# A filling queue that may go further into debt, and a reordered ending, in a GroupNorm, attention and projection kernel

## The chip, the core and the metric

The kernel runs on one NeuronCore of a Trainium2 chip, as one program. The metric is the device time of one execution in microseconds (us), the median of three runs. All the engines are named as the profile names them: PE is TensorE's matrix multiply, PEld its weight load, DVE is VectorE, ACT is ScalarE, POOL is GpSimd and SP is SyncE, which here only issues DMAs. A `q` behind an engine's name (SPq, ACTq) marks what its sequencer does itself, such as issuing a DMA, loading a register or branching. Times in the traces are counted from the start of the profiled span.

## The reference

```
x: (4, 512, 48, 48) float32, so batch 4, 512 channels, t = 2304 positions; 8 heads of 64 channels
hn  = group_norm(x, 32 groups) * scale + bias
qkv = einsum('oc,bchw->bohw', qkv_w, hn) + qkv_b, cast to float16
w   = softmax(einsum('bhct,bhcs->bhts', q*s, k*s)),  s = 1/sqrt(sqrt(64))
a   = einsum('bhts,bhcs->bhct', w, v), cast to float32
out = x + einsum('oc,bchw->bohw', proj_w, a) + proj_b
```

## The kernel before

**The stream.** A batch has four pairs of heads, so there are 16 pairs (g = 0 to 15). A pair's queries are cut into five blocks (j = 0 to 4), four of 512 columns and one of 256. A block is worked off in steps, six for a wide block and three for the narrow one, 27 steps for a pair and 432 in all (`stream`, n = 0 to 431). In step n, PE computes six score matmuls (`scores`, L955), twelve narrow ones in block 4, into three PSUM tiles `ps`; ACT turns them into `p` with three exponentials (L962); DVE adds `p` up (`add`, L1009); and PE multiplies the `p` of step n-2 with v (`values`, L980). PE runs its instructions in the order in which they were written, and so do ACT, DVE, POOL and SP. An engine waits for another one by semaphores alone, so that POOL may run a conversion long before or after the step of PE in which it was written.

**What is put between.** Everything else of PE's work, the projections to q, k and v (L709, L760) and the output projection (L844), is cut into pieces, which stand in one list `beside` in a fixed order. In each step `fill(n)` takes pieces from its front. A piece has a price in nominal microseconds, a first step `after` before which it may not be taken, and two marks, `first` and `last`, that say whether it begins or ends an accumulation chain. A whole chain carries both marks. At each call the credit grows by `rate`, the price of the pieces left over the steps left, and a piece's price is taken off when it is issued. A fill never begins a second chain after it has closed one.

```
        credit[0] = min(credit[0] + rate, 4.0)
...
            if us > 0.1 and credit[0] < us / 2:
                break
```

An output projection is a whole chain at 512/290 = 1.766 of those units (eight matmuls of 512 columns, `whi` and `wlo` for each of the four pairs). For the last three blocks of batch 3 it is cut in two: `FIRST`, the first three pairs (1.324 units), and `LAST`, the last pair alone (0.441 units, two matmuls). Four chains belong to a wide block, two to the narrow one. Before a block's first chain stands a piece of price 0, its conversion `att32`, which copies the attention of each pair c from float16 into the float32 tile `a32_c` that the chain's matmuls of that c read. Pairs 0 and 1 are copied by ACT (L838), pairs 2 and 3 by POOL (L836). There is one tile for each c, so that a copy waits for the chains of the block before that read it. The conversions of the last two blocks of batch 3 (`left_over`) have tiles of their own.

**Sums and division.** When a block's last `values` are done, its softmax sums go through DRAM: a copy, a DMA `sums` (L1051), on POOL the check of their range (L1070), on DVE a reciprocal (L1077), a DMA to a row (L1079), two broadcast DMAs `ib` (L1089), and on POOL the product `att` (`divide`, L1096), written six steps after the block's last one. POOL's queue takes that product, the checks and the conversions in the order in which they were written.

**The ending.** After step 431 the pieces that `beside` still holds are taken out as `ahead`, and the `LAST` chains not yet run are listed in `todo`: `ahead` first, then four of block 3 (tiles `rest`), then two of block 4 (tiles `held` and `last_av`). A chain of `ahead` is evacuated by a copy on ACT (L1424) and an add on POOL (L1427, in `finish`), the others by an add on DVE (L867). Each result is stored to `out` (L876), from SP or ACT in turn. POOL compares the block's sums with their range (L1456 to L1460), DVE and PE sum that up (L1470, L1471), and DVE writes `flag` (L1473). All five engines load the flag (L1488) and branch on it (L1494) past a fallback kernel, which with these inputs is not run. `expect_end` puts on an engine a register load of a zero (L923) and an announcement of that branch.

Of the kernel before, what the change touches and what calls it, by code (L numbers as in the profile page):

```python
# [17 lines left out]
ALU = mybir.AluOpType  # L18
# [8 lines left out]
P = 128  # L27
NC = C // P
# [439 lines left out]
def fast_path(  # L468
# [12 lines left out]
    nc = tc.nc  # L481
# [102 lines left out]
    def chain_bank(name):  # L584
        if alone[0]:
            return ps_s.tile([P, 2, QB], F32, tag="ps", name=name)[:, 0, :]
        return ps_w.tile([P, QB], F32, tag="pw", name=name)

    def small_bank(name):
        return ps_w.tile([P, QB], F32, tag="pw", name=name)  # L590
# [223 lines left out]
    def in_two(b, j):  # L814

        return b == B - 1 and j >= NQ - 3

    def left_over(b, j):

        return b == B - 1 and j >= NQ - 2  # L820

    beside_exps = range(NC // 2, NC)

    def att32(b, j, pairs=range(NC)):
        o, n = QBLOCKS[j]
        for c in pairs:
            if left_over(b, j):
                t = xpool.tile([P, n], F32R, tag=f"x{c}_{j}", name=f"a32_{b}_{j}_{c}")
            else:
                t = work.tile(  # L830
                    [P, QB], F32R, tag=f"a32_{c}", bufs=1, name=f"a32_{b}_{j}_{c}"
                )
            at32[b, j, c] = t[:, :n]
            source = atts[b * NPAIR + c][:, o : o + n]
            if c in beside_exps and len(pairs) > 1:
                nc.gpsimd.tensor_copy(at32[b, j, c], source)  # L836
            else:
                nc.scalar.copy(at32[b, j, c], source)  # L838
# [13 lines left out]
    FIRST, LAST = range(NC - 1), range(NC - 1, NC)  # L852
# [41 lines left out]
    def proj_pieces(b, j):  # L894

        def ahead(k):
            if k < len(proj_list) and not in_two(b, proj_list[k][0]):
                residual(b, *proj_list[k])  # L900

        def begin():
            att32(b, j, LAST if in_two(b, j) else range(NC))
            if j == 0:
                ahead(0)
                ahead(1)

        pairs = LAST if in_two(b, j) else range(NC)
        chains = [
            proj_piece(b, j, chunks, pairs, lambda k=k: ahead(k + 2))  # L910
            for k, (jj, chunks) in enumerate(proj_list)
            if jj == j
        ]
        return [piece(0.0, begin)], chains
# [6 lines left out]
    def expect_end(*engines):  # L921

        taken = nc.values_load(  # L923
            nothing[0:1, 0:1],
            engines=engines,
            min_val=0,
            max_val=1,
            skip_runtime_bounds_check_because="it is a constant",
        )
        tc.mark_branch_hint_location("fallback", taken, engines)  # L930
# [84 lines left out]
    def add_up(g, j, bank=None, more=False):  # L1015


        o, n = QBLOCKS[j]
        per = QB // n
        sl = bank  # L1020
        if bank is None:
            sl = ps_av.tile([P, QB], F32, tag="av", name=f"sl_{g}_{j}")
        steps = [
            (t, r, a)
            for t in acc.pop((g, j))
            for r in range(t.shape[1])
            for a in range(per)
        ]
        for i, (t, r, a) in enumerate(steps):
            for h in range(2):  # L1030
                lo = h * D
                nc.tensor.matmul(  # L1032
                    sl[lo : lo + D, :n],
                    ones16,
                    t[:, r, h, a * n : (a + 1) * n],
                    start=(i == 0 and (g, j) not in open_sums),
                    stop=(i == len(steps) - 1 and not more),
                )
        if more:
            acc[g, j] = []  # L1040
            open_sums.add((g, j))
        return sl
# [61 lines left out]
    beside = []  # L1104
# [34 lines left out]
    def do_tasks(room):  # L1139
        while tasks and tasks[0][0] <= now[0] and room > 0:  # L1140
            _, us, run = tasks.popleft()
            run()
            room -= us
# [42 lines left out]
    for b in range(B):  # L1186
# [20 lines left out]
        if b == B - 1:  # L1207
            put_qk(g + 3, 1)
            put_qk(g + 3, 0, range(NQ - 1))
            put_convert(old, 0)  # L1210
            put_qk(g + 3, 0, (NQ - 1,))

            ahead = [
                (residual, b, j, chunks)
                for j in (NQ - 2, NQ - 3, NQ - 1)
                for jj, chunks in proj_list
                if jj == j
            ]
            for j in range(NQ):
                put_proj(old, j, ahead)  # L1220
                if j + 1 < NQ:
                    put_convert(old, j + 1)

            for j in (NQ - 2, NQ - 3, NQ - 1):
                there = ends[(NG - 2) * NQ + j] + BEHIND + 6
                put_run(att32, b, j, FIRST, after=there)
                put_first(b, j)
            put_convert(b, 0)
            put_proj(b, 0)
            put_convert(b, 1)  # L1230
            put_proj(b, 1)
            put_convert(b, NQ - 3)
            put_proj(b, NQ - 3)
            continue
# [38 lines left out]
    for c in range(NC):  # L1273
# [10 lines left out]
        for i, chain in enumerate(chains):  # L1284
            evacuate = chain(c)
# [13 lines left out]
    credit = [0.0]  # L1299

    def issue():
        us, run = beside.pop(0)[:2]
        run()
        credit[0] -= us

    def fill(n):

        idle = beside and beside[0][4] and not beside[0][4]()
        if ended(n - 1):
            room = 1.1 if idle else 0.0
        elif ended(n - BEHIND - 1):
            room = 1.1 if idle else 0.5
        else:
            room = 2.4 if idle else 1.1
        do_tasks(room)
        rate, work = 0.0, 0.0
        for us, _, _, _, _, _, need in beside:  # L1320
            work += us
            left = min(need * per_pair, len(stream) - 4) - n
            rate = max(rate, work / max(left, 1))
        credit[0] = min(credit[0] + rate, 4.0)
        closed = False
        while beside:
            us, _, first, last, when, after, _ = beside[0]
            if after > n or (first and closed) or (when and not when()):
                break
            if us > 0.1 and credit[0] < us / 2:  # L1330
                break
            issue()
            closed = closed or last
# [21 lines left out]
    for n in range(end):  # L1355
# [10 lines left out]
        if summed:  # L1366

            fill(n)
# [10 lines left out]
        if not summed:  # L1379
            fill(n)  # L1380
        if n - BEHIND in soon:
            g, j = stream[n - BEHIND][:2]
# [9 lines left out]
    g, b, j = NG - 1, B - 1, NQ - 1  # L1392
    n = QBLOCKS[j][1]
    values(stream[-2])
    while loads:
        loads.popleft()[1]()
    check_sums(g, NQ - 2)
    att32(b, NQ - 2, LAST)

    def last_banks(name):  # L1400
        return ps_s.tile([P, 2, QB], F32, tag="ps", name=name)

    todo = [(jj, chunks) for jj, chunks in proj_list if in_two(b, jj)]
    todo = [k for k in todo if (k[0], k[1][0]) not in finished]
# [3 lines left out]
    add(stream[-1])  # L1408
    values(stream[-1])
    add_up(g, j, sl)  # L1410
    assert len(todo) == 8 and len(beside) == 2
    ahead, todo = todo[:2], todo[2:]

    def last_run(k, bank=None):
        return proj_run(b, *k, LAST, bank)

    def beyond(k, name, tag):
        bank = chain_bank(name)
        _, store = last_run(k, bank)
        t = xpool.tile([P, QB], F32, tag=tag, name=f"beyond_{name}")  # L1420
        xt = res[b, k[0], k[1][0]].rearrange("p m n -> p (m n)")

        def copy():
            nc.scalar.copy(t, bank)  # L1424

        def finish():
            nc.gpsimd.tensor_tensor(xt, t, xt, ALU.add)  # L1427
            store()

        return copy, finish  # L1430

    kinds = mybir.EngineType
    expect_end(kinds.DVE)
    inv = work.tile([P, QB], F32, tag="rows", name=f"inv_{g}_{j}")[:, :n]
    nc.vector.reciprocal(inv, sl[:, :n])
    o = QBLOCKS[j][0]
# [2 lines left out]
    copy, finish = beyond(ahead[0], "ahead_0", "x0_3")  # L1439
    copy()  # L1440
    expect_end(kinds.Pool)
    finish()
    ends_of = []
    for i, k in enumerate(todo[:NC]):
        if i % 2 == 0:
# [1 line left out]
        ends_of.append(last_run(k, banks[:, i % 2, :]))  # L1447
    expect_end(kinds.Activation)
    att32(b, j, LAST)
    copy, finish = beyond(ahead[1], "ahead_1", "x1_3")  # L1450
    copy()
    expect_end(kinds.PE, kinds.SP)

    every = fine.shape[1] + n
    fines = work.tile([P, QB], F32, tag="rows", name="fines")[:, :every]
# [2 lines left out]
    nc.gpsimd.tensor_scalar(ok, inv, 1.0 / SUM_MIN, None, ALU.is_le)  # L1458
    nc.gpsimd.tensor_tensor(fines[:, :n], fines[:, :n], ok, ALU.mult)
    nc.gpsimd.tensor_copy(fines[:, n:], fine)  # L1460
    finish()

    last_av = ps_av.tile([P, QB], F32, tag="av", name="last_av")
    for k, bank in zip(todo[NC:], (held[:, 1, :], last_av)):
# [1 line left out]
    good = small.tile([P, 1], F32, tag="good", bufs=1, name="good")  # L1466
    pf = small_bank("count")[:1, :1]
    for i, (evacuate, store) in enumerate(ends_of):
        if i == NC:
            nc.vector.tensor_reduce(good, fines, AX.X, ALU.add)  # L1470
            nc.tensor.matmul(pf, good, ones, start=True, stop=True)  # L1471
        if i == len(ends_of) - 1:
            nc.vector.tensor_scalar(flag, pf, P * every - 0.5, None, ALU.is_lt)  # L1473
        evacuate()
        store(nc.scalar if i % 2 else nc.sync)


@with_exitstack
# [54 lines left out]
```

## Time and profile before

| | us |
|---|---|
| median of three runs (1613.24 to 1616.65) | 1614.13 |
| the profiled execution's own time | 1613.1 |
| its span, from the first to the last instruction | 1611.4 |
| PE busy | 1581.6 |
| ACT busy | 1268.2 |
| DVE busy | 1136.2 |
| POOL busy | 321.5 |
| exponentials on ACT, mean of one | 1.025 |
| conversion of 128x512 on ACT, median from 1440 us on | 0.631 |
| conversion of 128x512 on POOL, median and longest from 1440 us on | 0.611 and 2.134 |

The profile is of one execution. Busy time is the union of an engine's instructions; a wide gap on PE means more than its share of busy time does, since nearly all of the span is PE's. An idle time is written in brackets in a timeline, with what ended it.

### The profile page before, as it was taken

The numbers are of one execution on the slowest core, as the hardware profiler recorded it, in microseconds if no ns is written. First come the engines' busy times: TensorE is split into PE (matmuls) and PEld (weight loads), VectorE is DVE, ScalarE is ACT, GpSimd is POOL, SyncE is SP. The second block draws the span as 40 slices with busy tenths as digits, with TensorE's granted clock in tenths as the row PEclk, the third lists the DMA queues.
The fourth block names the chain that finished last, engine by engine and source line by source line (L and its number), as shares of the span: only waits on it lengthen the run. The fifth ranks groups of instructions, "written<-read, shape, count | busy, mean of one in ns | idle before, by whom it ended". The sixth has DMA issues, their size and how long they took to land.

```text
span 1611.4 us, 28323 instructions
## 1 busy us (share of the span) xinstructions
PE 1581.6 (98%) x11500; PEld 695.2 (43%) x11500; DVE 1136.2 (71%) x1300; ACT 1268.2 (79%) x1362; POOL 321.5 (20%) x459
## 2 busy tenths in 40 slices
PE   7999999999999999999999999999999999999997
PEld 2533434443333534555333353455533334434554
DVE  6167668866666668986666666788666766667775
ACT  3077777888888888888887887887878888888895
POOL 1001112211121222312111121222212121222223
PEclk9999999999999999999999999999999999999998
DMA  7002020100000023511000001352100000016414
GB/s 219 4 14 67 11 66 22 18 14 11 14 18 14 10 68 119 158 50 28 14 12 18 14 12 57 100 157 79 27 16 14 14 15 14 12 31 183 129 53 140
DMA packets 94896, 82.10 MB, mean 51 GB/s; under 512 B 50852, under 2 KB 60964, under 8 KB 94756
## 3 DMA queue, kind: packets, MB, share of 16 engines
q1 hardware_dynamic: 92724, 78.35, 17.7%
q8 instruction: 92, 1.51, 0.4%
q10 hardware_dynamic: 1904, 1.84, 0.4%
q14 instruction: 48, 0.39, 0.1%
q0 software_dynamic: 128, 0.01, 0.0%
HBM read 60.70 MB, written 19.17 MB: 50 GB/s over the span
## 4 chain that ended last, share of the span: by engine, by line
PE 94%; DVE 2%; DMA 1%; ACT 1%; POOL 1%; issue 1%; SPq 0%; ACTq 0%; DVEq 0%; POOLq 0%
PE pqk L709 30%; PE ps L955 19%; PE av L980 19%; PE pv L760 16%; PE pr L844 8%; PE ps L709 1%; PE sl L1032 1%; ACT p L962 1%; DVE acc L1009 1%; DMA wqkv<-qkv_wT_dram 0%; POOL a L836 0%; DMA ib<-row 0%; DMA sums<-slx 0%; DMA row<-inv 0%; DMA x<-x_dram 0%
## 5 line engine op out<-in xcount | busy, mean ns | idle before, releaser
L962 ACT ACTIVATE p<-ps 128x1024 f16<-128x1024 f32 x1296 | 1233.4, 1025 | 311.6 <-PE ps L955 310.4
L1009 DVE TENSOR_TENSOR acc<-acc,p 128x3072 f16<-128x3072 f16 x270 | 485.9, 1800 | 70.8 <-ACT p L962 70.2
L709 PE MATMUL pqk<-x,wqkv 128*64 128x512 f32 (+1 forms) x2464 | 519.3, 551 | 0.0
L980 PE MATMUL av<-p,v 128*64 128x512 f16 (+1 forms) x2880 | 361.0, 364 | 0.4 <-DVE slx L1048 0.3
L955 PE MATMUL ps<-q,k 64*128 64x512 f16 (+1 forms) x2880 | 356.5, 358 | 1.7 <-ACT p L962 1.4
L760 PE MATMUL pv<-wqkv,x 128*64 128x256 f32 x2304 | 268.6, 380 | 0.0
L709 PEld LDWEIGHTS pqk<-x,wqkv 128*64 128x64 f32 x2464 | 169.0, 137 | 224.1 <-issue 166.7
L1070 POOL TENSOR_SCALAR in<-sums 128x8 f32<-128x8 f32 (+1 forms) x158 | 111.0, 703 | 718.9 <-DMA sums<-slx 712.4
L955 PEld LDWEIGHTS <-k 64*128 64x128 f16 x2880 | 106.3, 94 | 277.6 <-issue 228.8
L980 PEld LDWEIGHTS <-v 128*64 128x64 f16 x2880 | 132.0, 109 | 212.5 <-issue 168.4
L1096 POOL TENSOR_TENSOR att<-avx,ib 128x512 f16<-128x512 f32 (+1 forms) x78 | 122.8, 1575 | 446.1 <-DMA ib<-row 376.4
L760 PEld LDWEIGHTS pv<-wqkv,x 128*64 128x64 f32 x2304 | 160.6, 137 | 92.3 <-issue 4.5
L1009 DVE TENSOR_TENSOR acc<-p,p 128x3072 f16<-128x3072 f16 x79 | 138.2, 1749 | 0.0
L844 PE MATMUL pr<-a,whi 128*128 128x512 f32 (+1 forms) x310 | 122.3, 402 | 4.8 <-DVE q L719 2.1
L1012 DVE TENSOR_TENSOR acc<-acc 128x1024 f16<-128x1024 f16 x156 | 110.3, 707 | 5.3
L844 PE MATMUL pr<-a,wlo 128*128 128x512 f32 (+1 forms) x310 | 113.8, 375 | 0.0
L719 DVE TENSOR_SCALAR q<-pqk,bqkv 128x512 f16<-128x512 f32 (+1 forms) x79 | 54.8, 694 | 80.1 <-PE pqk L709 79.8
L719 DVE TENSOR_SCALAR k<-pqk,bqkv 128x512 f16<-128x512 f32 (+1 forms) x75 | 52.2, 696 | 77.9 <-PE pqk L709 77.8
L768 DVE TENSOR_TENSOR v<-pv,bv 128x512 f16<-128x512 f32 x72 | 49.7, 691 | 81.2 <-PE pv L760 80.9
L989 DVE COPY avx<-av 128x512 f32<-128x512 f32 (+1 forms) x79 | 50.6, 641 | 64.9 <-PE av L980 64.8
L871 DVE SCALAR_TENSOR_TENSOR r<-pr,bproj,r 128x512 f32<-128x512 f32 (+1 forms) x80 | 54.9, 695 | 46.2 <-PE pr L844 45.6
L844 PEld LDWEIGHTS pr<-a,whi 128*128 128x128 f32 x310 | 58.5, 189 | 43.8 <-issue 19.8
(79 smaller groups left out, 458.5 us busy)
## 6 DMA issues: line engine op xcount, KB each, us to landing
r<-x_dram SPq DMA_DIRECT2D x72, 256.0 KB, 3.2
out_dram<-r SPq DMA_DIRECT2D x69, 256.0 KB, 2.1
ib<-row SPq DMA_DIRECT2D x126, 128.0 KB, 3.1
x<-x_dram SPq DMA_DIRECT2D x62, 256.0 KB, 4.1
x<-x_dram SPq DMA_DIRECT2D x16, 128.0 KB, 4.8
sums<-slx SPq DMA_DIRECT2D x128, 2.0 KB, 2.1
ib<-row SPq DMA_DIRECT2D x30, 64.0 KB, 3.1
wqkv<-qkv_wT_dram SPq DMA_DIRECT2D x2, 768.0 KB, 6.9
```

The costliest lines, as they stand in the source:

```text
L709: nc.tensor.matmul(pw[0][lo : lo + D, :n], wqkv[:, c, w0 + lo : w0 + lo + D], hn[b, c, j], start=(c == 0), stop=(c == NC - 1),)
L719: nc.vector.tensor_scalar(qk[g][part][:, o : o + n], pw[0][:, :n], bqkv[:, col : col + 1], SCALE, ALU.add, ALU.mult,)
L760: nc.tensor.matmul(pw[0][lo : lo + D, a, :], hn[b, c, i * P // QB][:, at + lo : at + lo + D], wqkv[:, c, 2 * C + half * C // 2 :][:, : C / ...
L844: nc.tensor.matmul(ps[:, :n], w[:, c, bass.ts(m, P)], at32[b, j, c], start=(i == 0), stop=(i == len(steps) - 1),)
L871: nc.vector.scalar_tensor_tensor(xt[:, i], places[i], bias, xt[:, i], ALU.add, ALU.add)
L955: nc.tensor.matmul(ps[:, h, a * n : (a + 1) * n], kt[rows, bass.ts(i, P)], qt[rows, o : o + n], start=True, stop=True,)
L962: nc.scalar.activation(pt[:, r], ps, AF.Exp)
L980: nc.tensor.matmul(av[0][lo : lo + D, :n], vv[b, pr // 2][:, i, pr % 2 * P + lo : pr % 2 * P + lo + D], pt[:, r, h, a * n : (a + 1) * n], ...
L1009: nc.vector.tensor_tensor(t, before, pt, ALU.add)
L1012: nc.vector.tensor_tensor(t[:, 0], t[:, 0], t[:, r], ALU.add)
L1070: nc.gpsimd.tensor_scalar(t, sm, limit, None, op)
L1096: nc.gpsimd.tensor_tensor(atts[g][:, o : o + n], avx.pop((g, j))[:, :n], ibs.pop((g, j))[:, :n], ALU.mult,)
```

## The change

`att32` gives to POOL the copy of pair 3 that belongs to block 2 of batch 3 and was ACT's. In `fill`, a piece that is a whole chain is issued as soon as the credit is not negative; for the others the rule stays. The ending no longer asserts two chains in `ahead`, but one or two; where there is one, the second copy on ACT and add on POOL and its store fall away there, and where there are two, that store is put behind all the others. SP's announcement of the branch is written beside DVE's, ahead of the first store of the ending. In the last loop an evacuation and its store come before the sum of the comparisons, and the flag is written after the last evacuation.

```
-            if c in beside_exps and len(pairs) > 1:
+            if c in beside_exps and not (pairs == LAST and left_over(b, j)):
                 nc.gpsimd.tensor_copy(at32[b, j, c], source)
...
-            if us > 0.1 and credit[0] < us / 2:
+            if us > 0.1 and credit[0] < (0.0 if first and last else us / 2):
                 break
...
-    assert len(todo) == 8 and len(beside) == 2
-    ahead, todo = todo[:2], todo[2:]
+    ahead, todo = todo[: len(beside)], todo[len(beside) :]
+    assert len(todo) == NC + 2 and len(ahead) in (1, 2)
...
         def finish():
             nc.gpsimd.tensor_tensor(xt, t, xt, ALU.add)
-            store()
+            return store
...
-    expect_end(kinds.DVE)
+    expect_end(kinds.DVE, kinds.SP)
...
     expect_end(kinds.Pool)
-    finish()
+    finish()()
...
-    copy, finish = beyond(ahead[1], "ahead_1", "x1_3")
-    copy()
-    expect_end(kinds.PE, kinds.SP)
+    if len(ahead) > 1:
+        copy, later = beyond(ahead[1], "ahead_1", "x1_3")
+        copy()
+    expect_end(kinds.PE)
...
     nc.gpsimd.tensor_copy(fines[:, n:], fine)
-    finish()
+    if len(ahead) > 1:
+        store_ahead = later()
...
     for i, (evacuate, store) in enumerate(ends_of):
+        evacuate()
+        store(nc.scalar if i % 2 else nc.sync)
         if i == NC:
             nc.vector.tensor_reduce(good, fines, AX.X, ALU.add)
             nc.tensor.matmul(pf, good, ones, start=True, stop=True)
-        if i == len(ends_of) - 1:
-            nc.vector.tensor_scalar(flag, pf, P * every - 0.5, None, ALU.is_lt)
-        evacuate()
-        store(nc.scalar if i % 2 else nc.sync)
+    if len(ahead) > 1:
+        store_ahead()
+    nc.vector.tensor_scalar(flag, pf, P * every - 0.5, None, ALU.is_lt)
```

## The prediction

> **What bounds the kernel now.** I read the page's busy times and its chain first, then PE's timeline step by step from 1440 us on, since the queue's rule changes there, then the waits at each hole in PE, and last the instructions behind the last matmul.
>
> ```profile
> PE 1581.6 (98%) x11500; PEld 695.2 (43%) x11500; DVE 1136.2 (71%) x1300; ACT 1268.2 (79%) x1362; POOL 321.5 (20%) x459
> ...
> PE 94%; DVE 2%; DMA 1%; ACT 1%; POOL 1%; issue 1%; SPq 0%; ACTq 0%; DVEq 0%; POOLq 0%
> ```
>
> PE sets the time, and the change takes no matmul away. So it can gain only where PE stands still, and behind PE's end. Between 1440 and 1596 us PE has two large holes. Here is PE around 1463 us:
>
> ```profile
> 1462.98 0.39 PE L955 MATMUL ps<-q,k 64*128 64x512 f16 x2
> 1463.88 0.39 PE L955 MATMUL ps<-q,k 64*128 64x512 f16 x2 [0.51 <-ACT p L962]
> 1464.80 0.39 PE L955 MATMUL ps<-q,k 64*128 64x512 f16 x2 [0.53 <-ACT p L962]
> ```
>
> These are the scores of step 396. Step 395 holds scores and values alone, 1.52 us from 1461.46, whereas its three exponentials take 2.86 us: PE waits for ACT to free the tiles of `ps`. The other hole, with POOL's lines:
>
> ```profile
> 1486.69 1.27 POOL L1096 TENSOR_TENSOR att<-avx,ib 128x512 f16<-128x512 f32 x1 [8.49 <-DMA ib<-row]
> 1487.91 3.15 POOL L836 CAST a<-att 128x512 fp32r<-128x512 f16 x2
> 1490.10 0.50 PE L844 MATMUL pr<-a,whi 128*128 128x512 f32 x1 [1.18 <-POOL a L836]
> 1491.12 0.50 PE L844 MATMUL pr<-a,whi 128*128 128x512 f32 x1 [0.28 <-POOL a L836]
> ```
>
> A chain in step 402 waits for two copies, and these stood in POOL's queue behind a product that waited for its broadcast. Behind the last matmul I read what SP's queue waited for (us in all, times, longest) and the branch's rows (ns, then the first and last start):
>
> ```profile
> SPq L876 <- POOL r L1427: 2.8, 1, 2.8
> ```
>
> ```profile
> L1494 PEldq COMPARE_BRANCH  x1: 4107/4107/4107, 1603.3 to 1603.3; - x1
> ...
> L1494 ACTq COMPARE_BRANCH  x1: 68/68/68, 1604.6 to 1604.6; - x1
> L1494 SPq COMPARE_BRANCH  x1: 70/70/70, 1606.6 to 1606.6; - x1
> L1494 POOLq EVENT_SEMAPHORE  x1: 17/17/17, 1607.1 to 1607.1; - x1
> L1494 PEldq EVENT_SEMAPHORE  x1: 51/51/51, 1607.5 to 1607.5; - x1
> L1494 ACTq EVENT_SEMAPHORE  x1: 17/17/17, 1608.5 to 1608.5; - x1
> ```
>
> SP held finished results back until 1603.00. The semaphore lines are each engine's first act past the branch. SP's own comes at 1609.2 us, beside the landing of its last store (issued at 1604.4, 4.8 us to landing).
>
> **The credit.** I stepped the rule through the list in the code. It puts chains into the same steps as the trace's lines L709, L760 and L844, in every step to 430. At step 395 the credit is -0.8712. Left are 16 whole chains of block 0 to 4 of batch 2 (28.25 units), ten `FIRST` (13.24), eight whole ones of batch 3 (14.12), four `LAST` (1.77) and ten runs of 0.05 (0.50): 57.88 over 428 - 395 = 33 steps, a rate of 1.7539. The credit becomes 0.8827, and a chain asks 1.7655/2 = 0.8828: short by 0.0001, and the step stays empty. The new rule asks 0. Up to step 394 both rules issue the same; from 395 on every step takes what the next one took before. One `LAST` chain fewer is left: `ahead` has one entry, and the code for a second one (a copy on ACT, an add on POOL, the store to go last) is not run at all.
>
> **Step 395 filled.** Its chain takes 2.07 us (1459.39 to 1461.46 in step 394). ACT's exponentials end at 1464.75; the next scores come at 1462.98 + 2.07 = 1465.05 and wait for nothing. Scores of step 396: 2.14 us now (1462.98 to 1465.12), 0.75 elsewhere, **-1.39**.
>
> **Conversions a step earlier.** Block 2 of batch 2 is now converted in step 400 instead of 401, so it stands on POOL ahead of that product. The chain that frees its tiles ends at about 1483.3; two copies at 0.61 end at 1484.6; the next chain begins at 1484.8 and reads pair 2 first at 1485.7. The hole goes: 4.06 us (1487.72 to 1491.78) against 2.06, **-2.00**. What hides the copies is 1.5 us of scores and values. With DVE's adds beside them, as in the row above (2.13 for one), the 2.0 come back. Of the other moved conversions, only block 3's `FIRST` now comes right behind a product (step 410): by its row that broadcast lands 2.9 us into the step, the product takes 0.74 and the copy 0.61, 1520.5 us, and is read at 1522.3; nothing. ACT's two copies (1.26) come ahead of a 3.1 us step there: **+0.20** by ACT's 2.86 + 1.26 against 3.1 and the 0.8 us that its tiles reach ahead. From step 403 to 428 each step stands 2.07 - 1.39 - 2.00 = 1.32 us earlier, with one chain more done.
>
> **The late conversion on POOL.** It now reads a product that POOL itself has just written (1580.48 and 2.66 long; at most 1581.8 after the shift), and waits for the chain before, until 1581.7. Copy to 1582.4; read at 1583.2: **0**, slack 0.8. On ACT it stood ahead of exponentials (0.62). Bounds: -0.6, and +0.7 if it takes the 2.13 of the row above. [...] I take 0.61 because no `p` of block 3's last step is added on DVE, so DVE has only a PSUM evacuation then.
>
> **The last steps.** Steps 429 to 431 had one whole chain and two `LAST` (2.06 + 2 x 0.67); now three `LAST`, 2.01. Step 429 then takes PE 2.2 us against ACT's 2.86, and the third score tile of step 430 waits 0.65. To the end of `held`, 1596.27 us: -1.39 - 2.00 + 2.07 - 3.40 + 2.01 + 0.65 + 0.20 = **-1.9** us.
>
> **The ending.** From `held` to the flag (1602.72 + 0.14) the work keeps its order: reciprocal, product, four evacuations, POOL's three comparisons, sum. Flag at 1601.0. `held` is evacuated while DVE waited 0.87 for POOL, so the last evacuation ends at 1600.9 (before 1603.45) at no cost; the flag behind it still waits for the count, 0 to 0.1. SP's stores of `rest` and `held` go out by 1600, and only the flag's load (0.6) stands before its branch: 1601.65 instead of 1606.6. ACT: store at 1600.95, load, branch at 1602.0.
>
> Past the branch POOL takes 3.8 us, PE 4.1, ACT 3.9, SP 2.6, DVE 0.6. All had been announced (the L1529 hints behind the L923 loads), 5 to 7 us ahead, DVE's 9.8 us. So SP's earlier announcement, some 3.7 us by its queue, I cost at 0; its bounds are 0 and, since ACT comes as late, -1.0. ACT is past at 1605.95, PE at 1605.6, SP between 1604.2 and 1605.75, and the last store, 2.0 to 4.8 us after its issue, lands between 1603.0 and 1605.75. From SP's first semaphore to the end of the span are 1611.37 - 1609.21 = 2.16 us: 1606.4 to 1607.9. I take 1607.2, nearer to the longer rows since four engines fetch at once: **-4.2** on the span. The profiled execution would take 1613.1 - 4.2 = 1608.9; the median shown is 1.0 above it: 1609.9.
>
> [...]
>
> **Rivals.** *POOL's queue (slower).* Conversions in steps 396, 408, 410 and 428 now stand near a product or check. If the broadcasts land later than by these rows, each makes PE wait like step 402. It decides from 1.8 us at step 410 and 0.8 at 428; a broadcast took 5.0 us before step 402 and about 3 elsewhere. Four places at 2.0 to 2.5 against -4.2: +4 to +6, about 1619. Against it: loads of residuals made that one slow, and they are over by step 404. Chance 0.10.
>
> *The copies stay slow.* They meet DVE's adds wherever they stand, and step 401 waits as 402 did: the 2.0 us return, 1611.9, no difference. For it: 2.13 and 1.07 in the row. Against: the six other pairs from 1440 us on took 0.61 or less each. Chance 0.22.
>
> *The change does not do what it says.* 0.0001 may round the other way in my stepping, or two chains may remain; then only SP's order gains: ACT's branch resumes at 1608 and the end is 2.3 sooner, 1611.8. Chance 0.04.
>
> **How the numbers follow.** The sum above has 0.64; its own range is 1607.2 to 1611.5, from the branch's bounds, -1.0 for the announcement, +0.7 for the late copy and the runs' spread. About what a measurement of this kernel can tell from no change is 0.2%, 3.2 us: 1610.9 to 1617.4. Of the 0.64, 0.61 lie below that; with 0.02 of the second rival, faster has 0.63. The rest of the first case and of the two rivals near 1612 make 0.27, POOL's queue 0.10. The range reaches down to the first case's end and up to 1614.0, past the two middle cases, and leaves out POOL's queue and little else.
>
> **What would show it.** Step 395 has eight `pr` matmuls and step 396's scores no gap; no `pr` of step 401 waits for POOL's L836; POOL's 17 copies from 1440 us on become 18, ACT's 23 become 22; L1424 and the add of L1427 appear once; `held` ends near 1594.4, the flag stands near 1601, SP's branch near 1601.7, the span ends near 1607. I am wrong if another `pr` waits over 1 us for L836, if `held` ends after 1595.5, or if an engine needs over 5 us past its branch.

## The result, and the profile after

The kernel after took 1610.4 us (median of 20 runs, 1608.46 to 1613.69) against 1613.32 for the kernel before (20 runs, 1611.6 to 1617.17): a ratio of 0.998 [0.9973, 0.9987], 2.9 us less. A second set of 11 runs of the same kernel (`e5_after` below) gave 1609.58 against 1613.09, 0.9979 [0.997, 0.9988]. The profiled execution of after took 1612.11 us with a span of 1610.4, so it is one of the slower of its kernel; the profile of `e5_after`, with a span of 1608.3, stands beside it in what follows.

The page's busy times and the shares of its chain, after:

```profile
PE 1582.2 (98%) x11500; PEld 694.0 (43%) x11500; DVE 1136.0 (71%) x1301; ACT 1267.1 (79%) x1360; POOL 318.9 (20%) x459
...
PE 93%; DVE 2%; DMA 2%; issue 1%; ACT 1%; POOL 1%; SPq 0%; ACTq 0%; DVEq 0%; POOLq 0%
```

PE has as many matmuls and is as busy as before. ACT lost two instructions (the late copy and the second evacuation of `ahead`). So the gain has to be in the holes and in the end. PE's timeline of after, steps 395 and 396:

```profile
1461.59 0.82 PE L955 MATMUL ps<-q,k 64*128 64x512 f16 x6
1462.34 0.84 PE L980 MATMUL av<-p,v 128*64 128x512 f16 x6
1463.11 0.50 PE L844 MATMUL pr<-a,whi 128*128 128x512 f32 x1
...
1465.17 0.82 PE L955 MATMUL ps<-q,k 64*128 64x512 f16 x6
```

Step 395 now has its eight `pr` matmuls, and the six scores of step 396 stand in one line without a bracket: nothing waits for ACT. At the other hole, POOL's timeline from 1482 to 1491 us has two lines, and PE's step 402 has no bracket:

```profile
1483.18 1.17 POOL L836 CAST a<-att 128x512 fp32r<-128x512 f16 x2 [4.11 <-PE pr L844]
1487.36 1.27 POOL L1096 TENSOR_TENSOR att<-avx,ib 128x512 f16<-128x512 f32 x1 [3.01 <-DMA ib<-row]
```

The two copies that followed this product in the profile of before now run ahead of it, and are done by 1484.4. At the last matmuls, POOL's add no longer holds SP's queue. SP's waits from 1585 us on, before and then after (us in all, times, longest):

```profile
SPq L876 <- POOL r L1427: 6.2, 2, 3.3
...
SPq L1494 <- SPq L1494: 2.6, 1, 2.6
```

```profile
SPq L876 <- DVE r L867: 5.6, 4, 2.1
SPq L1497 <- SPq L1497: 4.8, 1, 4.8
...
SPq L876 <- POOL r L1427: 2.7, 1, 2.7
```

Of the two waits for L1427, 6.2 us together, one is left. It ends with POOL's only add at 1598.7, just ahead of the first evacuation of `rest` (1598.1 and 0.68 long), so it holds nothing back. Longer now is the wait of SP for itself past the branch (L1497, which was L1494): 4.8 us, 2.6 before. The branch's rows show it:

```profile
L1497 SPq EVENT_SEMAPHORE  x8: 17/17/17, 1608.3 to 1608.8; - x8
L1497 SPq COMPARE_BRANCH  x1: 70/70/70, 1603.4 to 1603.4; - x1
...
L1497 PEldq COMPARE_BRANCH  x1: 494/494/494, 1603.5 to 1603.5; - x1
L1497 ACTq COMPARE_BRANCH  x1: 68/68/68, 1604.0 to 1604.0; - x1
...
L1497 ACTq EVENT_SEMAPHORE  x1: 17/17/17, 1608.0 to 1608.0; - x1
L1497 POOLq EVENT_SEMAPHORE  x1: 17/17/17, 1608.2 to 1608.2; - x1
```

SP branches 3.2 us sooner than before (1606.6), but is past the branch only 0.9 us sooner (1609.2). POOL, which is off to the branch as early as before, needs 4.8 us where it needed 3.8.

The stages of the three profiles, each counted from the start of step 394, up to which the kernels are the same (us). The predicted column is the sum on record, stage by stage:

| stage | before | predicted change | after | `e5_after` |
|---|---|---|---|---|
| steps 395 and 396 | 6.48 | +0.68 | 7.17 (+0.69) | 7.17 (+0.69) |
| steps 397 to 402 | 23.84 | -2.00 | 21.90 (-1.94) | 21.92 (-1.92) |
| steps 403 to 428 | 91.27 | +0.20 | 92.72 (+1.45) | 91.48 (+0.21) |
| step 429 to the end of `held` | 13.21 | -0.74 | 12.53 (-0.68) | 12.53 (-0.68) |
| `held` to the flag | 6.60 | 0 | 6.62 | 6.61 |
| flag to the end of the span | 8.52 | -2.3 | 7.86 (-0.66) | 7.10 (-1.42) |
| sum | | -4.2 | -1.1 | -3.1 |

Two rows miss the forecast: steps 403 to 428 in the profile of after, and the last row in both. The experiments went after these two, and after the question which part of the change earns the time.

### The profile page after: what moved, and what is told of

Read it like the earlier page. It is cut to its first block, busy times and chain, and to the rows that moved or that the text cites. A ratio compares the mean times of both kernels' runs of the same rounds, so it can differ in the third digit from the quotient of the medians.

```text
span 1610.4 us, 28319 instructions
## 1 busy us (share of the span) xinstructions
PE 1582.2 (98%) x11500; PEld 694.0 (43%) x11500; DVE 1136.0 (71%) x1301; ACT 1267.1 (79%) x1360; POOL 318.9 (20%) x459
## 4 chain that ended last, share of the span: by engine, by line
PE 93%; DVE 2%; DMA 2%; issue 1%; ACT 1%; POOL 1%; SPq 0%; ACTq 0%; DVEq 0%; POOLq 0%
PE pqk L709 29%; PE ps L955 19%; PE av L980 19%; PE pv L760 16%; PE pr L844 8%; PE ps L709 1%; PE sl L1032 1%; DVE acc L1009 1%; ACT p L962 1%; DMA wqkv<-qkv_wT_dram 0%; DMA row<-inv 0%; DMA ib<-row 0%; POOL a L836 0%; DMA sums<-slx 0%; DVE r L871 0%
```

## The experiments

Each was timed in five rounds beside the kernel before. `e1_credit` to `e4_early_copy` shared a chip and the runs of before; so did `e5_after` to `e8_no_branch`, then `e9_early_words` and `e10_no_words`, then `e11_both` and `e12_before_words`.

### Which part gains, and the place of two copies

**The credit alone.** The kernel before with the new rule in `fill`. The `ahead` code was cut to its one remaining entry, and the rest is that of before.

```
-            if us > 0.1 and credit[0] < us / 2:
+            if us > 0.1 and credit[0] < (0.0 if first and last else us / 2):
```

> The credit rule alone: one chain left in ahead, so the second copy, add and store fall away by themselves, while the late copy stays on ACT, SP's announcement stays behind its store and the last loop keeps its old order. Theory 1 (the credit rule carries the change: it fills step 395, moves the copies of step 402 out of the way, and by leaving one chain it also frees SP's stores): both holes in PE gone (1.39 and 2.00 us), a new wait of about 1 us in step 411 for POOL's copy behind the product, SP's stores out by 1601.7; 2.0 to 2.6 us under the kernel before, ratio near 0.9985. Theory 2 (the rewritten ending carries it): the loop's gain is eaten by step 411 and the starved steps 430 and 431, under 0.8 us, ratio 0.9995 to 1.0.

Measured: 1610.24 us, 0.9984 [0.9975, 0.9993]. It has the whole gain of the change, within what can be told apart. One chain fewer is left for `ahead`, and that alone takes POOL's second add, and SP's wait for it, out of the ending: SP branches at 1601.2 and POOL at 1601.0, without any of the edits made to the ending.

**Everything but the credit.** The kernel after with the old rule.

```
-            if us > 0.1 and credit[0] < (0.0 if first and last else us / 2):
+            if us > 0.1 and credit[0] < us / 2:
```

> Everything of the change except the credit rule: two chains in ahead, their second store last on SP. Theory 1: step 396's scores and step 402's chain wait as before (0.5 + 0.5 and 1.18 + 0.28 us), the held tile still ends near 1596.2 us; SP's stores of rest and held go out up to 1.5 us sooner, but POOL's add still ends near 1603.0 and its store follows it, and the engines that miss the branch's target need 4 us: 0 to 1.5 us under the kernel before, ratio 0.999 to 1.0. Theory 2: 2 to 3 us under it, ratio near 0.998.

Measured: 1612.5 us, 0.9997 [0.9988, 1.0006]: no difference. PE waits at both holes as before, 1.1 us in all at the second where it was 1.5 (from 1440 us on):

```profile
PE ps L955 <- ACT p L962: 1.4, 3, 0.5
PE pr L844 <- POOL a L836: 1.1, 2, 0.8
```

Its ending gains nothing either: 8.75 us from the flag to the end, 8.52 before. SP does branch sooner (1604.9, against 1606.6 before), but ACT and POOL then need over 5 us past the branch (ACT 1604.3 to 1609.5, POOL 1604.1 to 1609.7).

**The late copy back on ACT.** The kernel after, with the condition in `att32` that of before.

```
-            if c in beside_exps and not (pairs == LAST and left_over(b, j)):
+            if c in beside_exps and len(pairs) > 1:
```

> The changed kernel with the late copy of pair 3 back on ACT. Theory 1: ACT waits for the chain of step 428 with it, copies for 0.62 us and starts step 429's exponentials 0.2 us later, so that the third score tile of step 430 waits 0.7 to 0.9 us instead of 0.52; 0.2 us slower than the changed kernel (0 to 0.6), ratio to the kernel before near 0.998. Rival (POOL's copy matters, since ACT is what bounds steps 429 to 431): 0.6 us or more slower, a wait of over 1.1 us in step 430.

Measured: 1610.03 us, 0.9982 [0.9973, 0.9991], no difference from `e5_after`. The trace does show a small one: from step 429 to the end of `held` it takes 12.78 us, and 12.77 in `e1_credit`, which has the copy on ACT too, against 12.53 with the copy on POOL. So the move is worth 0.25 us, which is too little for the runs' times to show. This profile also shows the collision of the next experiment: step 411, which took 3.11 us in `e5_after`, takes 3.92 here.

**Block 3's first conversion a step sooner.** In the profile of after, the excess of 1.24 us over `e5_after` in steps 403 to 428 is in the main one place: step 411 took 4.37 us against 3.11, the step behind it 0.24 less, and step 403 0.22 more. POOL's timeline at step 411:

```profile
1521.15 0.72 POOL L1096 TENSOR_TENSOR att<-avx,ib 128x256 f16<-128x256 f32 x1 [7.52 <-DMA ib<-row]
1521.82 2.14 POOL L836 CAST a<-att 128x512 fp32r<-128x512 f16 x1
```

and PE's, in step 411:

```profile
1522.63 0.40 PE L844 MATMUL pr<-a,wlo 128*128 128x512 f32 x1
1524.01 0.50 PE L844 MATMUL pr<-a,whi 128*128 128x512 f32 x1 [0.98 <-POOL a L836]
```

The same two instructions of POOL in `e5_after`:

```profile
1519.82 0.73 POOL L1096 TENSOR_TENSOR att<-avx,ib 128x256 f16<-128x256 f32 x1 [6.49 <-DMA ib<-row]
1520.49 0.61 POOL L836 CAST a<-att 128x512 fp32r<-128x512 f16 x1
```

and what DVE did meanwhile, in after and then in `e5_after`:

```profile
1521.21 2.28 DVE L1009 TENSOR_TENSOR acc<-acc,p 128x3072 f16<-128x3072 f16 x1
```

```profile
1520.92 1.80 DVE L1009 TENSOR_TENSOR acc<-acc,p 128x3072 f16<-128x3072 f16 x1
```

DVE's add begins 4.5 us into step 410 in every profile. In `e5_after` the copy was two thirds done by then, and took 0.61 us. In after the broadcast landed about 1 us later; the copy began 0.6 us into the add and ended 0.47 us behind the add's end (1523.96 against 1523.49), 2.14 us in all. The product began 4.4 us into step 410 there, 4.0 in `e3_copy_act` (copy 2.15), and 3.2 to 3.5 in the other profiles of this order, whose copies took about 0.6. The experiment writes this conversion into POOL's queue ahead of the product:

```
+                if j == NQ - 1:
+                    there = ends[(NG - 2) * NQ + NQ - 2] + BEHIND + 6
+                    put_run(att32, b, NQ - 2, FIRST, after=there)
...
-                put_run(att32, b, j, FIRST, after=there)
+                if j != NQ - 2:
+                    put_run(att32, b, j, FIRST, after=there)
```

> The changed kernel with the conversion of block 3's first three pairs put two chains earlier in the list (issued in step 409 instead of 410), so that POOL has it ahead of the product of step 410 that waits for its broadcast. Theory 1 (step 411's wait is POOL's order): the pr of step 411 waits for nothing, the 2.1 us copy of pair 2 becomes one of 0.6, step 412 begins 1.2 us sooner and the held tile ends 1.0 to 1.2 us sooner; about 1.1 us faster than the changed kernel, ratio to the kernel before near 0.9973. Rival (something else is late by as much: ACT's two copies, or the evacuations): the wait moves to the exponentials of steps 410 to 412 and the time stays, ratio near 0.998.

Measured: 1609.44 us, 0.998 [0.9971, 0.9989]. Step 411 took 3.11 us. In a later kernel with this order (`e11_both`) the product began 4.1 us into step 410, and step 411 still took 3.11. So the order removes the collision. Of the nine profiles with the order of after, two show it (after and `e3_copy_act`), so the profile of after was probably an unlucky one. The medians can't tell: that of `e4_early_copy` is 0.14 us under that of `e5_after`, and each ratio is uncertain by about 0.1%, 1.5 us.

### The ending, part by part

**The kernel after itself,** unchanged, for a second profile and a median on this chip:

> The changed kernel itself, for a second profile and a time beside the next three. If step 411's wait hangs on when the broadcast lands, as in the two profiles with and without it, it comes out at some other length, 0 to 1.3 us, here; if it is fixed by the order alone, it is 1.0 us again. Both holes of before stay gone, the third score tile of step 430 waits 0.5 us. 2.5 to 3.5 us under the kernel before, ratio 0.998.

Measured: 1609.58 us, 0.9979 [0.997, 0.9988], `held` at 1594.6. Its branch:

```profile
L1497 SPq EVENT_SEMAPHORE  x8: 17/17/17, 1606.2 to 1606.7; - x8
L1497 SPq COMPARE_BRANCH  x1: 70/70/70, 1602.2 to 1602.2; - x1
...
L1497 PEldq COMPARE_BRANCH  x1: 3723/3723/3723, 1602.3 to 1602.3; - x1
```

PE's branch took 3.7 us here and 0.5 in the profile of after, in one and the same program.

**SP's announcement beside PE's again:**

```
-    expect_end(kinds.DVE, kinds.SP)
+    expect_end(kinds.DVE)
...
-    expect_end(kinds.PE)
+    expect_end(kinds.PE, kinds.SP)
```

> The changed kernel with SP's announcement of the branch back beside PE's, behind SP's first store. Theory 1 (the earlier announcement brings nothing): SP is 2.6 to 4.9 us past its branch, as with it, and the time is within 0.5 us of the changed kernel's, or up to 1 us better, since the credit rule alone, with the announcement here, had 6.6 us from flag to end and not 7.3 to 7.9. PE, which crossed its branch in 0.5 us where it was announced alone and in 4 us where it was announced together with SP, needs 4 us again. Theory 2 (it brings what it was written for): SP needs 1 to 2 us more past its branch, 1 us slower.

Measured: 1609.67 us, 0.9976 [0.9967, 0.9986]. SP passed its branch in 3.9 us (1602.1 to 1606.0), against 4.0 in `e5_after`. The announcement's place in the ending makes no difference.

**The last loop in its old order,** the comparisons' sum and the flag ahead of the last evacuations:

```
-        evacuate()
-        store(nc.scalar if i % 2 else nc.sync)
...
+        if i == len(ends_of) - 1:
+            nc.vector.tensor_scalar(flag, pf, P * every - 0.5, None, ALU.is_lt)
+        evacuate()
+        store(nc.scalar if i % 2 else nc.sync)
...
-    nc.vector.tensor_scalar(flag, pf, P * every - 0.5, None, ALU.is_lt)
```

> The changed kernel with the last loop in its old order: the count before the evacuation of held, the flag before the last evacuation. Theory 1: the flag is written at the same place, since it hangs on POOL's comparisons; the last evacuation ends 0.6 us later and its store with it, but it lands before the engines are past their branches: 0 to 0.3 us. Theory 2: the last store sets the end, 0.6 us slower.

Measured: 1610.03 us, 0.9978 [0.9969, 0.9987]. No difference.

**No branch:** the loads of the flag, the announcements and the branch are gone.

```
-    fails = nc.values_load(
...
-    with tc.If(fails > 0, label="fallback"):
-        general_path(tc, *args)
```

> The changed kernel without the flag's loads, the announcements, the branch and the fallback behind it (the flag is still computed). Theory 1 (the engines' way past the branch sets the end): from flag to the end of the span 4.5 to 5.5 us instead of 7.3 to 7.9, bounded by the last store's landing and SP's list of semaphores; 2 to 3 us faster than the changed kernel, ratio to the kernel before 0.996 to 0.997. Rival (the landing of the last stores sets it): within 0.5 us of the changed kernel.

Measured: 1606.02 us, 0.9954 [0.994, 0.9967]. From the flag to the end are 3.73 us instead of 7.10. Five runs make this median. It is 3.6 us under that of `e5_after`, and the flag's loads with the branch are the cause, since the announcements alone cost nothing (`e10_no_words` below); the rest of the tail (last stores, the end of the program) stays.

### When an announcement is of use

In every kernel so far with a branch DVE, announced first, was past it in 0.6 us, and SP, ACT and POOL never in less than 2.6. The page of after lists two DMA queues of the kind `instruction` (packets, MB, share of 16 engines):

```profile
q8 instruction: 92, 1.51, 0.4%
...
q14 instruction: 48, 0.39, 0.1%
```

The packets of q8 are of 16 KB, those of q14 of 8 KB. The last of 8 KB ahead of the branch (1603.4) came at 1501.7, 1518.3, 1526.6 and 1595.7, the last of 16 KB at 1595.0 and 1599.7. So DVE's announcement (1593.2) had one more packet of 8 KB behind it, SP's, ACT's and POOL's, at 1595.9 to 1597.3, had none, and PE's (1597.1) had one of 16 KB. Which engine a packet is for the trace does not tell; the engines that the next expectation names are my inference from the packets' size and from the engine's place in its code.

**Announced earlier:** SP, ACT and POOL at step 400, PE at step 430, DVE where it was.

```
+        if n == 400:
+            expect_end(kinds.SP, kinds.Activation, kinds.Pool)
+        if n == 430:
+            expect_end(kinds.PE)
...
-    expect_end(kinds.DVE, kinds.SP)
+    expect_end(kinds.DVE)
```

and without the later three.

> The changed kernel with the announcements of SP, ACT and POOL put into step 400 and PE's into step 430, DVE's where it was. In the traces an engine's code arrives in blocks, and the last blocks before the branch were fetched near 1501 (POOL), 1518 (SP), 1526 (ACT), 1594 (PE) and 1594 us (DVE); only DVE was announced before its fetch, and only DVE crossed its branch in 0.6 us every time. Theory A (an announcement is served by the engine's next block fetch): all five engines are past the branch within 0.7 us, no block fetch lies between branch and first semaphore, from flag to the end of the span 4.0 to 5.0 us instead of 7.0 to 8.2, 2 to 3 us faster than the changed kernel, ratio to the kernel before near 0.996. [...]

Measured: 1607.15 us, 0.9966 [0.9954, 0.9978]. The branch:

```profile
L1498 SPq EVENT_SEMAPHORE  x8: 17/17/17, 1601.2 to 1602.7; - x8
L1498 SPq COMPARE_BRANCH  x1: 70/70/70, 1600.7 to 1600.7; - x1
...
L1498 PEldq COMPARE_BRANCH  x1: 504/504/504, 1600.8 to 1600.8; - x1
...
L1498 POOLq EVENT_SEMAPHORE  x1: 17/17/17, 1601.3 to 1601.3; - x1
L1498 ACTq EVENT_SEMAPHORE  x1: 17/17/17, 1601.4 to 1601.4; - x1
```

All five engines are past it within 0.6 us, and no packet of the two instruction queues comes between the branch and that: the next one comes at 1601.8. The span ends 4.52 us after the flag.

**No announcements at all,** the branch kept:

```
-    expect_end(kinds.DVE, kinds.SP)
...
-    expect_end(kinds.Pool)
...
-    expect_end(kinds.Activation)
...
-    expect_end(kinds.PE)
```

> The changed kernel with no announcement at all, the branch kept. Theory A: only DVE loses by it (its crossing takes 3 to 5 us like those of the others), and as SP, ACT and POOL take as long anyway, from flag to end 7 to 8 us as in the changed kernel: within 0.5 us of it, ratio to the kernel before near 0.998. Theory B (the late announcements do help those engines): 1 us or more slower than the changed kernel.

Measured: 1609.6 us, 0.9979 [0.997, 0.9988], as after. The row that tells is DVE's:

```profile
L1493 DVEq COMPARE_BRANCH  x1: 72/72/72, 1600.3 to 1600.3; - x1
...
L1493 DVEq EVENT_SEMAPHORE  x1: 21/21/21, 1604.3 to 1604.3; - x1
```

Without its announcement DVE needs 4.0 us where it needed 0.6. So the announcements do work, and those of the kernel after bring nothing to SP, ACT and POOL; removing them costs nothing. What the early ones changed is both the place ahead of the 8 KB packets (those at 1501.7 to 1526.6 in after) and the time ahead of the branch, over 100 us instead of 3.6 to 8.4. For SP, ACT and POOL no run separates the two. For PE the time ahead does not decide: announced 5.1 to 6.6 us ahead, it passed in 0.5 us in five profiles and in 3.7 to 4.1 in four.

**Both,** the early announcements with the early conversion of `e4_early_copy`:

> Both improvements on the changed kernel: the announcements of SP, ACT, POOL and PE put ahead of their last block fetches, and block 3's first conversion issued in step 409. Expected 0 to 0.3 us better than the announcements alone (the collision in step 411 came in two of ten profiles of the order it removes, at 0.8 and 1.2 us): 1606.5 to 1607.5, ratio to the kernel before near 0.996. Rival: the copies of ACT that now fall into step 409 cost as much elsewhere, no difference.

Measured: 1607.16 us, 0.997 [0.9958, 0.9982]. Its edit is the sum of the two above. It shows no gain over `e9_early_words`, timed in another set (0 to 0.3 us were expected). The two are the best of those that keep the branch: `e9_early_words` is 2.4 us under `e10_no_words` of the same set, and both are some 6 us under the kernel before.

**The kernel before with the early announcements:** the edit of `e9_early_words` on the old credit and ending.

> The kernel before, with the announcements alone put ahead of the last block fetches. Its ending has a second bound, the store behind POOL's last add, so that SP issues its last store 1.5 us behind the flag and it lands 6 us behind it. Theory 1 (two bounds lie side by side in the kernel before, and the credit rule took away only the one): all engines past the branch in 0.6 us, but from flag to end still 7.5 to 8.5 us, 0 to 1 us faster than the kernel before, ratio 0.9995 to 1.0. Rival (the branch alone bounds both kernels): 2.5 us faster, ratio 0.9985.

Measured: 1612.23 us, 0.9997 [0.9988, 1.0006], no difference. PE, ACT and POOL are past the branch in 0.5 us, and yet from the flag to the end are 8.71 us. SP's waits from 1585 us on:

```profile
SPq L876 <- POOL r L1432: 6.7, 2, 3.5
...
SPq L1495 <- SPq L1495: 3.0, 2, 2.4
```

SP's last store still stands behind POOL's second add; its packets run until 1606.6, and the second of SP's two waits past the branch ends at 1607.0. The span ends 2.4 us behind the last packet of a store here, in the profile of before, and in `e1_credit`, `e9_early_words` and `e11_both` (2.3 to 2.4), but 4.2 us or more behind it in after and the other profiles with a branch. So SP's store set the end of before, with the branch close by (ACT is past it at 1608.5, SP goes on at 1609.2), and to take away the branch's cost alone gives nothing. To take the store away gave 0.7 us in the profile of after and 1.9 in that of `e1_credit`, from flag to end. The change takes the store away (by the credit); the early announcements then take the branch. This profile shows one thing more: step 402 took 4.11 us here, 5.59 in the profile of before and 3.58 in after. The product on POOL had begun at 1484.74 (1486.69 there), and PE waited 0.27 us for the copies, although one of them still took 2.13. So that hole, too, grows and shrinks with the landing of a broadcast: this slow copy began 0.48 us into an add of DVE's, the one of before 0.94, and both ended 0.47 us behind the add.

## Why the prediction was right, and where it missed

**The credit and step 395: right.** The traces show chains in the steps that the stepping of the rule gave, up to step 430. Steps 395 and 396 changed by +0.69 against +0.68, and one entry of `ahead` is left. `e1_credit` and `e2_no_credit` together show that this rule is the cause of the gain.

**Conversions a step earlier: right, with one place more.** Step 402 lost its 2.0 us (5.59 to 3.58), and the two copies moved ahead of its product took 0.61 and 0.62 in after. Step 411 was the exception. The prediction had seen its copy come behind a product, and cleared it by a slack of 1.8 us. The copy has to begin before DVE's add does, 4.5 us into the step, to take the 0.61 of `e5_after` and not the 2.14 of after; it comes 0.67 us behind the product's begin, which may thus lie 3.8 us into step 410, where the row of before gave 2.9. The true slack is 0.9. The missed step was to take a copy at 0.61 that would then begin inside DVE's next add. So the rival *POOL's queue* is real at one of its four places, in two profiles of nine, for 1.26 and 0.81 us of step 411 rather than 2.0. The reason given against it does not hold: in the profile of before seven loads of residuals (L811) come from step 404 to step 410, 1496.6 to 1518.8 us, and the two broadcasts at step 410 took 3.5 and 3.9 us there, 4.7 and 5.2 in after. The +0.20 for ACT's copies there was right: 0.24, from 6.80 us for steps 411 and 412 of `e5_after` against 6.56 for the same work before.

**The late copy: nearly.** Expected 0, measured 0.25 us of gain: on ACT it had delayed the exponentials that step 430 waits for. It ran at 1583.59 for 0.61 us, with DVE on an evacuation, as taken. What a copy took depended on whether DVE's add had begun ahead of it. Of the 206 copies of 128x512 on POOL from 1440 us on in all fourteen profiles, 36 began inside one of DVE's adds into `acc`, and each ended 0.47 to 0.50 us behind that add. The other 170 took 0.60 to 0.62, also those that began inside an evacuation from PSUM, as the late copy did. So the reason given for 0.61 holds.

**The last steps: right,** -0.68 against -0.74. The wait that was to come is PE's in step 430:

```profile
1586.72 0.40 PE L955 MATMUL ps<-q,k 64*128 64x256 f16 x4 [0.52 <-ACT p L962]
```

**The ending: right in its mechanism, 0.9 us or more too good.** The flag came where `held` put it, and SP's store no longer ended last. Mis-sized was the term from the flag to the end: -2.3 predicted, -1.42 in `e5_after`, -0.66 in after, and over six profiles of this ending, or of it with one edit undone, between -0.3 (`e7_old_order`) and -1.5 (`e6_late_word`). Two durations were taken from a trace in which SP came last and alone. The flag's load, in after:

```profile
L1491 SPq TENSOR_LOAD <-flag x1: 749/749/749, 1602.5 to 1602.5; - x1
L1491 POOLq TENSOR_LOAD <-flag x1: 775/775/775, 1602.6 to 1602.6; - x1
```

It was 0.30 for POOL before, 0.62 for SP. And SP's way past the branch, 2.6 us in the row of before, became 4.0 and 4.9 when SP, POOL and ACT went at once. The prediction had said that four engines fetch at once, and then took 6.2 us from flag to end, between 5.4 and 6.9; the runs gave 7.1 and 7.9, above the upper bound too. In after four packets of 8 KB and one of 16 KB came past the branch within 0.2 us (1605.1 to 1605.3); which engine each was for is not shown, and that engines slow each other there was not tried by itself. What is shown is that POOL, SP and ACT each took 3.7 us or more past the branch in both profiles of this kernel.

A second cause is possible. Behind SP's branch the next packet of an instruction queue came 1.2 us later in `e5_after`, 1.8 in after and 1.8 in `e7_old_order`. In the latter two, and not in `e5_after`, a store on SP took 1.6 and 2.0 us to issue while a packet of 16 KB ran beside it, and packets of stores still ran for 1.0 us behind that first packet. So stores under way may account for part of the spread between the profiles; no run separates this.

**The announcement: right at 0.** `e6_late_word` shows no difference. One thing was not known then: in both places the announcement comes behind the start of the last 8 KB packet ahead of the branch (1595.9 against 1595.7 in after; 1600.0 against 1596.1 in before, where it stands beside PE's). That this is the reason is my estimate, and no run shows it apart from the time ahead.

**By its own conditions.** That `held` should end by 1595.5 and no `pr` wait over 1 us for L836 held in `e5_after` (1594.6, no such wait). In the profile of after `held` ended at 1595.9, one of the three signs of being wrong, with a wait of 0.98, which is the collision. No engine needed over 5 us past its branch in either; the longest was SP's 4.9. The time on record, 1609.9, is 4.2 us under its median of before, and the runs show 2.9 and 3.5. That the measured 1610.4 lies only 0.5 from it is in part luck: the gain was put 1.3 us too high in the one set, and the median of three runs of before, from which it was counted, was 0.8 above that of twenty.

## What to carry to other kernels

When a filling rule moves work by one step, follow each moved copy to what runs beside it on the other engines, and give its slack as the distance to that, not to its reader. When two bounds end within a microsecond of each other, taking one away can show little or nothing by itself, so measure the second alone (`e8_no_branch`, `e12_before_words`) before sizing the first. A duration read from an engine that acted alone can be too short once others do the same thing at the same time: SP's way past the branch took 2.6 us in before, where it came last, and 4.0 and 4.9 us where it went with POOL and ACT.

## What the runs showed of the hardware

- With SP, ACT and POOL announced at step 400, PE at step 430 and DVE where it was, all five engines passed the branch in 0.5 to 0.6 us (`e9_early_words`, `e11_both`). Announced 3.6 to 8.4 us ahead, SP, ACT and POOL took 2.6 us or more, and 3.3 to 4.0 with no announcement at all (`e10_no_words`). PE's, announced late, passed in 0.5 us in after, `e2_no_credit`, `e3_copy_act`, `e4_early_copy` and `e7_old_order`, and in 3.7 to 4.1 in before, `e1_credit`, `e5_after` and `e6_late_word`. In the first five a 16 KB packet came 1 to 3 us after PE's announcement, in the others only after its branch. What decides that is open.
- A copy of 128x512 on POOL takes 0.61 us. Begun inside one of DVE's float16 adds, it ended 0.47 us behind that add: 2.14 us when begun 0.61 into an add of 128x3072 that took 2.28, 0.70 when begun 1.52 into one of 1.75. The other way round, when an add of 128x3072 began beside a running copy, the add ended 1.60 to 1.69 us behind the copy (1.62 in `e5_after`). Why the two distances are so constant is not shown.
- A branch taken at the end, with the flag's load, cost 3.6 us of time (`e8_no_branch` against `e5_after`), and 1.1 with the announcements of `e9_early_words` (1607.15 against 1606.02 for `e8_no_branch`, in different sets of runs).
